# In layer 1 of a convolution-and-Mamba stack, ScalarE copies a projection right after its matmuls, and the pause comes after the copies

## The chip, the core and the metric

The kernel runs on one NeuronCore of one Trainium2 chip. A core has five engines that each work through their own instructions in order: TensorE (PE, matrix products; its weight loads are listed as PEld), VectorE (DVE), ScalarE (ACT), GpSimd (POOL) and SyncE (SP, which here issues the DMAs). They wait for each other by semaphores. The metric is the device time of one execution in microseconds (us), lower is better.

## The reference

The input x has the shape (8, 192, 56, 56). Four layers follow, each of the form x = x + layer(group_norm(x)):

```
x = x + L0(gn(x))    # involution, 5x5 taps made from the pixel itself
x = x + L1(gn(x))    # layer norm, three Mamba slices of 64 channels (d_inner 512), layer norm, projection
x = x + L2(gn(x))    # Mamba, d_inner 384
x = x + L3(gn(x))    # Mamba, d_inner 384
```

The change is in layer 1. There the 192 channels are split into three slices of 64, all with the same weights, and each slice of each image is a sequence of 3136 tokens:

```
xi, z = split(x @ in_proj_W.T)                 # 512 each
xc  = silu(causal_conv4(xi) + conv_b)
dbl = xc @ x_proj_W.T                          # 4 for dt, 16 for B, 16 for C
dt  = softplus(dbl[:, :4] @ dt_proj_W.T + dt_proj_b)
h   = h * exp(dt * A) + (dt * xc) * B          # 16 states per channel, along the sequence
y   = (sum over states of h * C + xc * D) * silu(z)
out = y @ out_proj_W.T
```

dbl, the projection of xc, is what the changed step makes: 36 rows that hold B, C and the 4 inputs of dt.

## The kernel before

A sequence is cut into 7 chunks of T = 448 tokens. In layer 1 a **job** is one slice (0, 1, 2) of one chunk of one image: 8 x 7 x 3 = 168 jobs. A job has 4 groups j of 128 channels with 4 **units** each (a unit q has 4 of the 16 states of each channel), 16 units in all, numbered m = 0 to 15 in the job. Layers 2 and 3 have 56 jobs of 12 units each. For each unit (loop at the end of `ssm_layer`):

- ACT makes the decays exp(dt * A) in PSUM, in two halves of two instructions each (`decays`, L749). There are two decay buffers, so the first half for unit k + 1 can't begin before the first scan of unit k is over.
- The inputs (dt * xc) * B are made by POOL for odd units (`inputs_by_pool`, L768) and by DVE for even ones (`inputs_by_vector`, L774), which reads a row b that PE spreads over the partitions (`spread_b`, L743).
- DVE runs two scans (`scan`, L778), one per half. ACT then copies the last column away for the next chunk (`keep`, L782).
- POOL multiplies with C in place (`readout`, L787). It can't begin before the keep has read the last column.
- PE adds up the states (`reduce`, L796; at the first unit of a group also xc * D, L793). DVE multiplies with silu(z) once per group (`gated`, L812).

While job i runs through its units, the background work of job i + 1 is laid between them: convolution and input projection on PE with ACT copies (L613), silu of xc and z (L616, L597, with table loads), the output projection of job i - 1 (L1076, copied by ACT in L1081), the **projection of xc** on PE (`xproj`, L621, four matmuls of two passes each), its two copies on ACT (`xproj_out`: L625 into `dbl`, L626 into `parts` as bf16), what bf16 left over of B (`left_of_b` L632 and L633, `part_of_b` L637), the matmuls of dt with their copies (`delta` L655, `delta_out` L660), the stores of B and C (`rows_out` L643), softplus (L663), and so on.

This background work is a list of `Step`s. A step has matmuls, a rest (the copies), a `left` and a cost. `Steps.run` first calls the rests that are pending until only `left` of them remain; then it issues the step's matmuls and puts its rest among the pending ones, or, for a step without matmuls, calls its rest at once. So a rest is issued when a later step flushes it. `pause` has left = 9 and flushes nothing; `flushed` has left = 0 and flushes all; both issue nothing themselves.

`places` deals the steps out over the 32 places of a job: places 2m and 2m + 1 belong to unit m. The steps come in stretches with bounds. The stretch that begins with the projection of xc has places 8 to 17 when the job being prepared is of slice 0 or 2, and 8 to 13 when it is of slice 1. At each place the room is the average of the cost that is left; steps are put there while room is over 0, each step takes its cost off it, and what a step took too much is a debt at the next places. In the unit's code the even place stands ahead of the first scan and of the first half of the decays for the next unit:

```
bg.run(plan[2 * m])
nothing(k - 3, more > 0)
load_when_free(k)
scan(k, 0)
if k + 1 < n_units:
    decays(k + 1, 0)
```

The odd place stands ahead of the second scan, the keep and the second half of the decays. `nothing` (L802) issues dummy matmuls that add zeros to the unit's sum, up to three in a unit, except in the last unit of a group; `more` is 3 less the rounded-up cost of those steps of the unit's two places that have matmuls.

Of the kernel before, what the change touches and what calls it, by code (L numbers as in the profile page):

```python
# [49 lines left out]
def pause(cost=1.0):  # L50
    return Step(None, lambda: None, 9, cost)


def settle(cost=2.0):

    step = Step(None, lambda: None, 0, cost)
    step.settles = True
    return step


def flushed(cost=1.0):

    return Step(None, lambda: None, 0, cost)
# [23 lines left out]
def conv_mamba_stack(ctx: ExitStack, tc: tile.TileContext, a, out):  # L87
# [16 lines left out]
    def mm_tile():  # L104
        return banks.mm.tile([128, 512], F32, tag="mm", name="mm")
# [481 lines left out]
    def table_block(ops):  # L587
        ops()
        nc.scalar.preload_act_table_set(EXP_SET)  # L589

    def with_gates(ops, u):


        def all_ops():
            ops()
            if u is not None:
                nc.scalar.activation(u.zs, u.zs, AF.Silu)  # L597

        table_block(all_ops)

    def project_steps(pool, w, u, conv_mm, conv_cost, running=None, meanwhile=()):


        nd, rank = w.nd, w.rank
        nk = rank + 2 * NS

        def conv(j):
            if j == 0:
                u.xc = pool.tile([128, nd, T], F32, tag="xc", name="xc", bufs=2)
            u.cps[j] = conv_mm(j)  # L610

        def conv_out(j):
            nc.scalar.activation(u.xc[:, j, :], u.cps[j][:, :T], AF.Identity, bias=w.convb[:, j : j + 1])  # L613

        def silu():
            with_gates(lambda: nc.scalar.activation(u.xc, u.xc, AF.Silu), running)  # L616

        def xproj():
            u.ps = mm_tile()
            for j in range(nd):  # L620
                nc.tensor.matmul(u.ps[:nk, :T], lhsT=w.xproj[:, j, :], rhs=u.xc[:, j, :], start=(j == 0), stop=(j == nd - 1))  # L621

        def xproj_out():
            u.dbl = pool.tile([44, T], F32, tag="dbl", name="dbl", bufs=2)
            nc.scalar.copy(u.dbl[:nk, :], u.ps[:nk, :T])  # L625
            nc.scalar.copy(u.parts[:NS, :], u.ps[:NS, :T])  # L626


        def left_of_b(m):
            u.left[m] = mm_tile()  # L630
            rows = NS if m == 0 else 96
            nc.tensor.matmul(u.left[m][:NS, :T], lhsT=ident[:NS, :NS], rhs=u.dbl[:NS, :], start=True, stop=False)  # L632
            nc.tensor.matmul(u.left[m][:NS, :T], lhsT=minus[:rows, m, :], rhs=u.parts[:rows, :], start=False, stop=True)  # L633

        def part_of_b(m):
            p0 = 32 * m + 32
            nc.scalar.copy(u.parts[p0 : p0 + NS, :], u.left[m][:NS, :T])  # L637

        def rows_out():

            u.bc = dram.tile([NS, 2, T], F32, tag="bc", name="bc", bufs=3)
            for c in range(2):
                nc.sync.dma_start(out=u.bc[:, c, :], in_=u.dbl[c * NS : c * NS + NS, :])  # L643

        def row_in(c, q):

            u.rows[c, q] = pool.tile([128, T], F32, tag=f"rows{c}", name="rows", bufs=4)
            by_n = u.bc.rearrange("(n q) c t -> n q c t", q=NQ)[:, q, c]
            nc.sync.dma_start(out=u.rows[c, q], in_=by_n.unsqueeze(0).to_broadcast([32, 4, T]))

        u.rows, u.row_in = {}, row_in

        def delta(j):
            u.dps[j] = mm_tile()
            nc.tensor.matmul(u.dps[j][:, :T], lhsT=w.dtw[:, j * 128 : (j + 1) * 128], rhs=u.dbl[:nk, :], start=True, stop=True)  # L655

        def delta_out(j):
            if j == 0:
                u.dt = pool.tile([128, nd, 2, T], F32, tag="dt", name="dt")
            nc.scalar.activation(u.dt[:, j, 0, :], u.dps[j][:, :T], AF.Identity, bias=w.dtb[:, j : j + 1])  # L660

        def softplus():
            table_block(lambda: nc.scalar.activation(u.dt[:, :, 0, :], u.dt[:, :, 0, :], AF.Softplus))  # L663

        def x_again(j):
            u.xps[j] = mm_tile()
            nc.tensor.matmul(u.xps[j][:, :T], lhsT=ident, rhs=u.xc[:, j, :], start=True, stop=True)  # L667

        def dtx(j):
            nc.vector.tensor_mul(u.dt[:, j, 1, :], u.dt[:, j, 0, :], u.xps[j][:, :T])  # L670

        def store(j):
            u.ops[j] = dram.tile([128, 2, T], F32, tag="ops", name="ops", bufs=8)
            nc.sync.dma_start(out=u.ops[j], in_=u.dt[:, j])

        u.ops, u.cps, u.dps, u.xps, u.left = {}, {}, {}, {}, {}
        deltas = [Step(lambda j=j: delta(j), lambda j=j: delta_out(j), 1) for j in range(nd)]

        stores = [Step(lambda j=j: x_again(j), lambda j=j: dtx(j), 1 if j > 1 else 9) for j in range(nd)]
        return (  # L680
            [Step(lambda j=j: conv(j), lambda j=j: conv_out(j), 1, conv_cost) for j in range(nd)]
            + [settle()], [Step(None, silu, 0, 0.3, block=True), *meanwhile] + [Step(xproj, xproj_out, 9, nd)] * (nd == 3),
            ([Step(xproj, xproj_out, 0, nd), pause()] if nd == 4 else [Step(None, lambda: None, 2, 3.5)])
            + [Step(lambda: left_of_b(0), lambda: part_of_b(0), 0, 1.3)] + deltas[:1] + [Step(None, rows_out, 2)] + deltas[1:2]
            + [Step(lambda: left_of_b(1), lambda: part_of_b(1), 1, 1.3)] + deltas[2:]
            + [settle()], [Step(None, softplus, 0, 0.3, block=True)] + stores[:2],
            [Step(None, lambda: store(0), 0)] + stores[2:3] + [Step(None, lambda: store(1), 1)]
            + stores[3:] + [Step(None, lambda j=j: store(j), nd - 1 - j) for j in range(2, nd)]
        )
# [295 lines left out]
    def mamba_jobs(pool, w):  # L985
# [3 lines left out]
        for ck in cks:  # L989
# [50 lines left out]
            for i in range(3):  # L1040

                def prepare(u, *beside, i=i, ck=ck, norm=norm):
                    def conv_mm(j):
                        pm = mm_tile()
                        for k in range(2):
                            nc.tensor.matmul(  # L1046
                                pm[:, :T], lhsT=w.inconv[:, k, j * 128 : (j + 1) * 128],
                                rhs=ck.xs[:, i, 2 - 2 * k : 2 - 2 * k + T], start=(k == 0), stop=(k == 1),
                            )
                        return pm  # L1050

                    convs, *others, stores = project_steps(pool, w, u, conv_mm, 2, *beside)
                    if i == 0:
                        stores = stores + [Step(None, lambda: chunks.fetch_next(ck), 2)]
                        if ck.place == 0:
                            convs = norm() + convs
                    return convs, *others, stores
# [34 lines left out]
    def dense_jobs(pool, w, layer):  # L1092
# [3 lines left out]
        for ck in cks:  # L1096
# [11 lines left out]
            def prepare(u, *beside, c=c, ck=ck, in_mm=in_mm):  # L1108
# [17 lines left out]
                def conv_mm(j):  # L1126
# [3 lines left out]
                    return pm  # L1130

                convs, *others = project_steps(pool, w, u, conv_mm, 4, *beside)
                return (
                    [Step(None, gnorm, 2)]
# [116 lines left out]
```

## Time and profile before

| what | us |
|---|---|
| median of 3 runs | 24955.37 (24948.31 to 24965.5) |
| the profiled execution, its time | 24963.74 |
| the profiled execution, its span | 24961.9 |
| layer 1 in it, first to last scan instruction and what hangs on them | 1607 to 17034 |
| busy in the span: PE | 21153.9 |
| DVE | 22616.8 |
| ACT | 17043.4 |
| POOL | 23597.2 |

The profile is of one execution. A page gives the busy time of each engine, and groups of instructions by line of the kernel: so many, busy time, mean duration in ns, and the idle time just ahead of them with what ended it. A timeline lists instructions in order of time: start and duration in us, engine, line, operation, what it writes and reads, and in brackets how long the engine had been idle before it and what released it. Rows of the same kind are merged (x3 is three instructions in a row). A fp32 matmul appears as two passes. A list of waits gives, for engine and line, what was waited for, the sum, the count and the longest. A row of stretches gives busy time (and number of instructions) of PE, PEld, DVE, ACT and POOL, then PE's granted clock (1.00 is full speed), the share of the DMA engines, and GB/s.

The costliest lines are DVE's scans (L778, 15905.1 us busy), POOL's readouts (L787, 14739.8), ACT's decays (L749, 10254.0) and POOL's inputs (L768, 8038.6).

### The profile page before, as it was taken

What the parts mean: (1) busy time and instruction counts of PE and PEld (TensorE: products, weight loads), DVE (VectorE), ACT (ScalarE), POOL (GpSimd) and SP (SyncE); (2) the same over time, 40 slices, a digit from 0 to 9 for tenths busy, and PEclk for the clock granted to TensorE, in tenths of its full rate; (3) what the DMA queues carried; (4) which work ended last, traced back from release to release, by engine and by line L of the source; (5) the groups of instructions that cost most, each with busy time, mean ns of one, the idle gap of its engine ahead of it and who ended that gap; (6) DMA issues with size and microseconds to landing.
All of it is one profiled execution on the core that took longest, in us unless ns stands there. A gap on an engine that the chain in (4) does not pass through costs nothing.

```text
span 24961.9 us, 237862 instructions
## 1 busy us (share of the span) xinstructions
PE 21153.9 (85%) x74220; PEld 6587.3 (26%) x74220; DVE 22616.8 (91%) x15661; ACT 17043.4 (68%) x32578; POOL 23597.2 (95%) x6996
## 2 busy tenths in 40 slices
PE   8988888888888888888888888888888888888888
PEld 2222222222222222222222222222333332333332
DVE  8989999999999999999999999997999998999998
ACT  2247777777767777777777777776777776777776
POOL 6679999999999999999999999998999998999999
PEclk9987777777777777777777777778888888888888
DMA  4433333333333333333333333333444443444443
GB/s 110 110 108 123 121 123 123 121 121 124 124 122 121 123 123 123 122 123 122 121 125 123 121 122 122 125 122 112 140 132 139 139 138 121 140 141 143 142 141 127
DMA packets 1184899, 3132.97 MB, mean 126 GB/s; under 512 B 163756, under 2 KB 446404, under 8 KB 1183496
## 3 DMA queue, kind: packets, MB, share of 16 engines
q1 hardware_dynamic: 1180824, 3116.70, 38.2%
q8 instruction: 582, 9.54, 0.2%
q14 instruction: 693, 5.68, 0.1%
q10 hardware_dynamic: 2800, 1.06, 0.0%
HBM read 2399.92 MB, written 555.55 MB: 118 GB/s over the span
## 4 chain that ended last, share of the span: by engine, by line
DVE 35%; PE 24%; ACT 17%; issue 11%; POOL 7%; DMA 4%; SPq 1%; DVEq 0%; POOLq 0%; ACTq 0%
DVE uhg L778 24%; ACT da L749 8%; DVE uhg L774 7%; PE y L796 4%; POOL uhg L787 4%; PE mm L655 4%; DMA rows<-bc 2%; PE y L802 2%; POOL uhg L768 2%; ACT L589 2%; PE y L793 2%; PE mm L632 2%; DMA rep<-ops 2%; ACT zs L597 1%; PE mm L429 1%
## 5 line engine op out<-in xcount | busy, mean ns | idle before, releaser
L778 DVE TENSOR_TENSOR_SCAN uhg<-da,uhg 128x898 f32<-128x898 f32 x8064 | 15905.1, 2009 | 1279.9 <-ACT da L749 1276.6
L787 POOL TENSOR_TENSOR uhg<-uhg,rows 128x1792 f32<-128x1792 f32 x4032 | 14739.8, 3676 | 275.4 <-ACT carry L782 267.4
L749 ACT ACTIVATE da<-rep,k 128x448 f32<-128x448 f32 x16128 | 10254.0, 636 | 1669.3 <-DVE uhg L778 1291.5
L768 POOL TENSOR_TENSOR uhg<-rep,rows 128x1792 f32<-128x1792 f32 x2016 | 8038.6, 3987 | 481.6 <-DMA rows<-bc 212.7
L796 PE MATMUL y<-uhg,k 128*32 128x448 f32 x32256 | 4780.6, 669 | 757.6 <-POOL uhg L787 755.3
L774 DVE TENSOR_TENSOR uhg<-rep,b 128x1792 f32<-128x1792 f32 x2016 | 4025.5, 1997 | 468.8 <-PE b L743 424.1
L782 ACT COPY carry<-uhg 128x4 f32<-128x4 f32 x4032 | 787.3, 195 | 3547.9 <-DVE uhg L778 3464.2
L793 PE MATMUL y<-xc,w_d 128*128 128x448 f32 x2016 | 1485.7, 832 | 1390.0 <-DVE zs L812 1388.3
L802 PE MATMUL y<-w_d,k 128*128 128x448 f32 (+1 forms) x5276 | 2496.8, 581 | 0.0
L796 PEld LDWEIGHTS y<-uhg,k 128*32 128x32 f32 x32256 | 695.9, 117 | 3858.8 <-issue 2203.8
L655 PE MATMUL mm<-dbl,w_dt 36*128 36x448 f32 (+1 forms) x2016 | 1501.2, 858 | 155.0 <-ACT k L637 155.0
L1102 PE MATMUL mm<-v,w_in 96*128 96x448 f32 x2688 | 1464.8, 677 | 170.1 <-ACT zs L694 71.1
L802 PEld LDWEIGHTS y<-w_d,k 128*128 128x128 f32 x5276 | 1050.9, 214 | 1480.4 <-issue 1452.5
L1046 PE MATMUL mm<-xs,k 128*128 128x448 f32 x2688 | 1229.7, 592 | 112.4 <-ACT zs L694 100.5
L1129 PE MATMUL mm<-xin,w_conv 128*128 128x448 f32 x2688 | 1077.9, 543 | 1.0 <-ACT xin L696 0.9
L441 DVE TENSOR_TENSOR prod<-mm,shifted 128x448 f32<-128x448 f32 x1680 | 928.6, 611 | 141.2 <-PE mm L429 63.5
L632 PE MATMUL mm<-dbl,k 16*16 16x448 f32 x1120 | 687.8, 702 | 422.7 <-ACT dbl L625 422.7
L667 PE MATMUL mm<-xc,k 128*128 128x448 f32 x2016 | 971.4, 592 | 30.8 <-DVE dt L670 29.7
L793 PEld LDWEIGHTS y<-xc,w_d 128*128 128x128 f32 x2016 | 443.3, 258 | 2056.5 <-DVE zs L812 1392.8
L1064 PE MATMUL mm<-xs,k 64*128 64x448 f32 x1344 | 861.6, 750 | 109.0 <-ACT zs L694 109.0
L743 PE MATMUL b<-k,k 96*128 96x448 bf16 x2016 | 832.2, 413 | 126.8 <-DVE uhg L774 126.6
L449 POOL TENSOR_TENSOR x<-x,one 96x448 f32<-96x448 f32 x560 | 631.1, 1134 | 265.9 <-DVE one L441 248.4
(138 smaller groups left out, 19672.2 us busy)
## 6 DMA issues: line engine op xcount, KB each, us to landing
rep<-ops SPq DMA_DIRECT2D x4032, 448.0 KB, 5.9
ops<-dt SPq DMA_DIRECT2D x1008, 448.0 KB, 3.3
rows<-bc SPq DMA_DIRECT2D x1792, 224.0 KB, 6.2
shifted<-xpad SPq DMA_DIRECT2D x672, 179.0 KB, 4.5
xg<-stream SPq DMA_DIRECT2D x168, 336.0 KB, 3.8
xr<-stream SPq DMA_DIRECT2D x168, 336.0 KB, 5.3
stream<-xr SPq DMA_DIRECT2D x112, 336.0 KB, 3.4
xs<-xg SPq DMA_DIRECT2D x224, 112.0 KB, 2.3
```

Of the source, the lines that this page charges most:

```text
L632: nc.tensor.matmul(u.left[m][:NS, :T], lhsT=ident[:NS, :NS], rhs=u.dbl[:NS, :], start=True, stop=False)
L655: nc.tensor.matmul(u.dps[j][:, :T], lhsT=w.dtw[:, j * 128 : (j + 1) * 128], rhs=u.dbl[:nk, :], start=True, stop=True)
L749: nc.scalar.activation(t[:, 64 + 449 * r : 512 + 449 * r], reps[k // NQ][:, 2 * h + r, 0, :], AF.Exp, scale=w.neg_a[:, j * NR + 2 * h + r, ...
L768: nc.gpsimd.tensor_mul(uhg[k][:, :, 1:], reps[k // NQ][:, :, 1, :], b)
L774: nc.vector.tensor_mul(uhg[k][:, :, 1:], reps[k // NQ][:, :, 1, :], b)
L778: nc.vector.tensor_tensor_scan(v, banks.da[h][:, 63:961], v, 0.0, ALU.mult, ALU.add)
L787: nc.gpsimd.tensor_mul(v, v, us[i].rows[1, q].unsqueeze(1).to_broadcast([128, NR, T]))
L793: nc.tensor.matmul(ys[k // NQ][:, :T], lhsT=w.dd[:, j, :], rhs=us[i].xc[:, j, :], start=True, stop=False)
L796: nc.tensor.matmul(y[32 * r : 32 * r + 32, :T], lhsT=fold, rhs=uhg[k][:, r, 1:], start=False, stop=(q == NQ - 1))
L802: nc.tensor.matmul(ys[k // NQ][:, : nd * 112], lhsT=zeros, rhs=w.dd.rearrange("p j e -> p (j e)")[:, : nd * 112], start=False, stop=False,)
L1046: nc.tensor.matmul(pm[:, :T], lhsT=w.inconv[:, k, j * 128 : (j + 1) * 128], rhs=ck.xs[:, i, 2 - 2 * k : 2 - 2 * k + T], start=(k == 0), st ...
L1102: nc.tensor.matmul(pm[:, :T], lhsT=w.inw[:, k, m * 128 : (m + 1) * 128], rhs=ck.v[:, k, :], start=(k == 0), stop=(k == NCT - 1),)
```

## The change

In the list that `project_steps` returns, for the four-group form of layer 1 alone, the step of the projection gets cost 1.0 in place of 4, a `flushed()` of cost 1.0 is put behind it, and the pause behind that gets cost 3.0 in place of 1.0:

```
-            ([Step(xproj, xproj_out, 0, nd), pause()] if nd == 4 else [Step(None, lambda: None, 2, 3.5)])
+            ([Step(xproj, xproj_out, 0, 1.0), flushed(), pause(3.0)] if nd == 4 else [Step(None, lambda: None, 2, 3.5)])
             + [Step(lambda: left_of_b(0), lambda: part_of_b(0), 0, 1.3)] + deltas[:1] + [Step(None, rows_out, 2)] + deltas[1:2]
             + [Step(lambda: left_of_b(1), lambda: part_of_b(1), 1, 1.3)] + deltas[2:]
             + [settle()], [Step(None, softplus, 0, 0.3, block=True)] + stores[:2],
```

`flushed` calls the pending rest, here the two copies L625 and L626, which before were called by the next step with matmuls, the first `left_of_b`. The sum of the three costs is 5 both times. No operation of the computation is added, left out or changed; since `more` is worked out from the costs, the number of `nothing` matmuls beside the projection follows from them.

More of the change, by code (lines that the diff above doesn't have):

```diff
@@ L682, in project_steps @@
             + [settle()], [Step(None, silu, 0, 0.3, block=True), *meanwhile] + [Step(xproj, xproj_out, 9, nd)] * (nd == 3),
-            ([Step(xproj, xproj_out, 0, nd), pause()] if nd == 4 else [Step(None, lambda: None, 2, 3.5)])
+            ([Step(xproj, xproj_out, 0, 1.0), flushed(), pause(3.0)] if nd == 4 else [Step(None, lambda: None, 2, 3.5)])
             + [Step(lambda: left_of_b(0), lambda: part_of_b(0), 0, 1.3)] + deltas[:1] + [Step(None, rows_out, 2)] + deltas[1:2]
```

## The prediction

> **What bounds the kernel now.** I read the page first, then layer 1 alone (1607 to 17034 us), because the edited line runs for `nd == 4`, which only layer 1 has. First the page's busy line, then layer 1 as one stretch (PE, PEld, DVE, ACT, POOL, granted clock, DMA), then the waits of POOL and DVE inside it:
>
> ```profile
> PE 21153.9 (85%) x74220; PEld 6587.3 (26%) x74220; DVE 22616.8 (91%) x15661; ACT 17043.4 (68%) x32578; POOL 23597.2 (95%) x6996
> ...
> 1607.00:17034.00 15427.00, 12939.79 (x40112) 3728.61 (x40112) 14128.32 (x8554) 10953.91 (x20959) 15070.15 (x4046) 0.77 0.36 122
> ...
> POOL uhg L787 <- ACT carry L782: 220.9, 195, 4.0
> ...
> DVE uhg L778 <- ACT da L749: 742.3, 394, 3.8
> DVE uhg L774 <- PE b L743: 369.0, 222, 2.7
> ```
>
> POOL is busy 15070 of 15427 us, so at most some 357 us can be won here. DVE, at 14128, follows closely, and POOL already waits 220.9 us for scans (through the small keep copy L782). So the two engines limit each other in turn: what makes scans late costs nothing while POOL still has readouts to do, and everything once it has run out. I read POOL's lag from the timelines as the start of each readout L787 minus the end of its second scan, by unit m of the 16 in a job and by the slice (0, 1, 2) that the job prepares. The medians are 5.5 us at m = 5 and 2.7 at m = 10 in slice-0 jobs, but 0.31 (the smallest that occurs: none left) at m = 14 of slice 1 and at m = 4, 10 and 12 of slice 2. The lag is used up twice in every three jobs.
>
> Then the place itself, in a job that prepares slice 2 (timelines of PE, ACT, DVE and POOL; start, duration; the value in brackets is idle time before):
>
> ```profile
> 5017.43 4.99 PE L1076 MATMUL mm<-zs,w_out 128*64 128x448 f32 x8
> 5022.35 0.96 PE L796 MATMUL y<-uhg,k 128*32 128x448 f32 x8
> 5023.24 3.20 PE L621 MATMUL mm<-xc,w_x 128*36 128x448 f32 x8
> ...
> 5023.07 0.52 ACT L1081 COPY y<-mm 64x448 f32<-64x448 f32 x1
> 5023.81 1.31 ACT L749 ACTIVATE da<-rep,k 128x448 f32<-128x448 f32 x2 [0.22 <-DVE uhg L778]
> 5025.05 0.18 ACT L757 COPY uhg<-carry 128x4 f32<-128x4 f32 x1
> 5025.72 0.20 ACT L782 COPY carry<-uhg 128x4 f32<-128x4 f32 x1 [0.49 <-DVE uhg L778]
> ...
> 5028.97 0.52 ACT L625 COPY dbl<-mm 36x448 f32<-36x448 f32 x1
> 5029.40 0.52 ACT L626 CAST k<-mm 16x448 bf16<-16x448 f32 x1
> ...
> 5021.74 5.86 DVE L778 TENSOR_TENSOR_SCAN uhg<-da,uhg 128x898 f32<-128x898 f32 x3 [2.84 <-ACT da L749]
> ...
> 5025.02 7.30 POOL L787 TENSOR_TENSOR uhg<-uhg,rows 128x1792 f32<-128x1792 f32 x2
> ```
>
> This is unit 4. The projection of xc (L621) ends at 5026.4; its copies (L625, L626) come 2.5 us later, when nobody has to wait for PE. The decays at 5023.81 are what the third scan of the DVE row, which starts at 5025.59, needs.
>
> **The change part by part.** *Where the copies go.* In `places` (L821) the stretch has 13.9 of cost, before (4 + 1 + 8.9) and after (1 + 1 + 3 + 8.9). Over 10 places (slices 0 and 2) room is 1.39 at place 8, over 6 places (slice 1) 2.32. The projection now takes 1.0 of it, so room is left and `flushed()` falls into the same place 8. So the copies are issued straight behind their matmuls, ahead of the decays for unit 5 on ACT. From place 11 (10 in slice 1) on the plan is what it was, since the sums are equal.
>
> *What ACT pays.* Both copies keep their duration: L625's start to L626's end is 0.95 us. They now wait for L621, and behind them are queued the decays of unit 5, the small copy L757 and the keep of unit 4 (L782). Slice-2 example: L621's end 5026.42, release 0.04 (L633's end to L637 at another place of this job), copies 0.95, decay pair to scan 1.34 (5020.40 to 5021.74): the scan starts at 5028.75 instead of 5025.59, D = 3.16 us late. When PE is quicker, D shrinks. In a slice-0 job:
>
> ```profile
> 3455.33 3.22 PE L1076 MATMUL mm<-zs,w_out 128*64 128x448 f32 x8
> 3459.37 3.20 PE L621 MATMUL mm<-xc,w_x 128*36 128x448 f32 x8
> ...
> 3462.49 0.52 ACT L1081 COPY y<-mm 64x448 f32<-64x448 f32 x1
> ```
>
> L621 is done at 3462.57, ACT at 3463.01, so only the copies themselves are in the way: 3463.01 + 0.95 + 1.34 = 3465.30 against 3465.04, D = 0.26. I took D so for 166 jobs. Slice 0 (55): 0.26 in 29, 3.16 in 23, 81.7 us in all. Slice 1 (55): 0.26 to 2.86, mostly 0.3 to 1.6, 59.7. Slice 2 (56): 3.16 in 50, 161.1.
>
> *What sets D is PE's clock.* L1076 takes 3.22 us at a granted clock of 1.00 (stretch 3455.3 to 3458.5) and 4.99 at 0.64 (5017.4 to 5022.4). The job of 3364.73 shows a half-clock stretch behind a wait of 1.61 us:
>
> ```profile
> 3360.79 1.02 PE L793 MATMUL y<-xc,w_d 128*128 128x448 f32 x2 [1.61 <-DVE zs L812]
> 3361.74 1.37 PE L796 MATMUL y<-uhg,k 128*32 128x448 f32 x8
> ...
> 3364.73 5.31 PE L1076 MATMUL mm<-zs,w_out 128*64 128x448 f32 x8
> ```
>
> [...]
>
> *What is won.* PE's wait at L632 for L625 (350.2 us over layer 1) goes. But the next step on that chain, the second delta matmul, waits for L637, which stands on ACT behind the decays of unit 7, and these wait for a scan. So that chain moves with DVE and gives nothing back in slices 0 and 2. In slice 1 the left-over copies now also leave ACT's queue ahead of unit 6's decays, and DVE's later waits there come from PE (L774 for L743, 64.0 us at m = 8) and from the softplus behind PE-bound copies (64.8 at m = 8): about 2.3 us a job that covers D up to that. I take slice 1 at nothing. Its bounds: a gain of 1.4 us a job (the second delta and left matmuls at full instead of half clock, 2 x 0.9 less 0.4), -77, and the whole of D, +60.
>
> *Two more dummy matmuls.* `nothing` (L802) is asked for by `more`, which counts the costs of steps with matmuls: at m = 4 that was 4 (none), it is 1 (two). Each is 1.02 us at full clock, 167 x 2.04 = 341 us of PE. They lie where PE waited for L625 or stands idle before the second delta; the b row (L743) for DVE is later by one of them, 5027.7 against a reader at 5030.7. At nothing, then; without that cover, DVE would be at most 1.0 us later a job, 170 us. `pause(3.0)` issues nothing. On SP the two stores of dbl (L643) can go 2.5 us sooner; the next load behind them waits for other things.
>
> *POOL.* The readout of unit 4 waits for the delayed keep. In slice 2 it starts 0.28 us after the keep does (median), so POOL stands for nearly D at once. In slice 0 the 2.4 us of lag at m = 10 takes up some of D, until m = 14 of the next job, where none is left.
>
> *Sum.* 81.7 + 161.1 + 0 = 243 us on the profiled execution's 24963.74 gives 25207; the median shown is 8 us lower, so 25200. Bounds: D at 0.26 in all jobs of slices 0 and 2 (29 us) with the slice-1 gain (-77): -48; D at 3.16 in all of them (351) and 60 in slice 1: +411. I take the phases as the trace has them, since the waits that cause them lie ahead of the edited place.
>
> **The rivals.** (a) POOL's lag hides slice 0 as well: 161 us, 25115. For it: 5.5 us of lag at m = 5. Against: none at m = 14 of the next job. (b) Faster: the dummies and the closed gap at L632 keep PE at full clock through units 5 to 9. DVE's waits at m = 8 to 10 add up to 523 us over the three slices; less D at 0.26 (43 us) this could give 480, and half of the waits gives 24955 - 262 + 43 = 24735. It decides if PE's idle time ahead of the second delta stays under 1.6 us, the shortest that a half-clock stretch followed in the rows above. Against: the first left matmul now ends at about 5031.9, the delta can't start before 5038.6, and between them are 2.3 us of work: 4.4 us idle. In the slice-0 job it comes to 3.9. (c) The change does what its name says: copies one place behind, after unit 5's decays. Then no scan is late; only the keep is, by 2 us, POOL waits sooner instead of later in slice 2, and the time stays near 24955. Against: the room of 0.39 at place 8. (d) The added lateness puts the out projection on half clock in nearly all jobs, slice 1 too: the upper bound, 25365.
>
> **How the numbers follow.** Forecast 0.66, (a) 0.16, (b) 0.08, (c) 0.05, (d) 0.05. A change of 0.2% (50 us) is about what can be told from none. Slower: forecast, (a) and (d), 0.66 + 0.16 + 0.05 = 0.87, less 0.02 for forecasts with quick phases, 0.85; same: (c) and those 0.02, 0.07; faster: (b), 0.08. The range leaves out (b), (c) and the far ends: 25000 to 25380.
>
> **What would show it.** L621 of layer 1 named as what ACT waits for before L625, some 250 us in all, at most 3.0 a time; DVE's wait for L749 up from 742 to about 1000; POOL's wait for L782 up from 221 to 400 or more; L802 up by some 670 instructions; L632's wait for L625 gone. Wrong, if POOL's waits rise much less than DVE's (then (a)), if layer 1's granted clock rises well above 0.77 (then (b)), or if L625 comes after unit 5's decays (then (c)).

## The result, and the profile after

The changed kernel takes 25087.99 us (median of 4 runs, 25058.35 to 25099.4) where the kernel before takes 24957.25 (4 runs): 1.005 times as long, 95% interval 1.0035 to 1.0065. It is slower by 131 us, inside the range of 25000 to 25380, at about half of the forecast loss of 243.

The page's busy lines, then layer 1's waits (ACT, DVE, POOL and PE, from 1607 to 17160 us: what waited, for what, sum, count, longest) of the changed kernel:

```profile
PE 21030.2 (84%) x74888; PEld 6618.8 (26%) x74888; DVE 22633.5 (90%) x15661; ACT 17027.2 (68%) x32578; POOL 23610.2 (94%) x6996
...
ACT dbl L625 <- PE mm L621: 111.2, 85, 2.9
...
DVE uhg L778 <- ACT da L749: 866.5, 499, 3.8
DVE uhg L774 <- PE b L743: 345.5, 237, 2.7
...
POOL uhg L787 <- ACT carry L782: 331.2, 259, 3.7
...
PE mm L655 <- ACT k L637: 642.7, 167, 5.5
```

No engine has more work that matters: DVE and POOL are as busy as before. What grew are waits, in the order that the prediction walked through: ACT now waits for the projection (L621) ahead of its copy L625, DVE's scans wait 124 us more for the decays, POOL waits 110 us more for the keeps. PE's wait at L632 for L625 (350.2 us before) is gone, and a wait for L637 ahead of the delta matmuls has grown in its place (155.0 before).

One unit 4 in a job that prepares slice 2 (timelines of PE, ACT, DVE and POOL):

```profile
3664.17 1.02 PE L793 MATMUL y<-xc,w_d 128*128 128x448 f32 x2 [1.95 <-DVE zs L812]
...
3668.45 4.91 PE L1076 MATMUL mm<-zs,w_out 128*64 128x448 f32 x8
3673.30 0.96 PE L796 MATMUL y<-uhg,k 128*32 128x448 f32 x8
3674.18 3.20 PE L621 MATMUL mm<-xc,w_x 128*36 128x448 f32 x8
3677.31 1.02 PE L802 MATMUL y<-w_d,k 128*128 128x448 f32 x2
...
3674.07 0.52 ACT L1081 COPY y<-mm 64x448 f32<-64x448 f32 x1
3677.42 0.53 ACT L625 COPY dbl<-mm 36x448 f32<-36x448 f32 x1 [2.83 <-PE mm L621]
3677.85 0.52 ACT L626 CAST k<-mm 16x448 bf16<-16x448 f32 x1
3678.27 1.29 ACT L749 ACTIVATE da<-rep,k 128x448 f32<-128x448 f32 x2
...
3672.74 3.94 DVE L778 TENSOR_TENSOR_SCAN uhg<-da,uhg 128x898 f32<-128x898 f32 x2 [2.84 <-ACT da L749]
3679.67 2.03 DVE L778 TENSOR_TENSOR_SCAN uhg<-da,uhg 128x898 f32<-128x898 f32 x1 [2.98 <-ACT da L749]
...
3679.86 3.68 POOL L787 TENSOR_TENSOR uhg<-uhg,rows 128x1792 f32<-128x1792 f32 x1 [3.10 <-ACT carry L782]
```

This is the predicted chain. L625 stands straight behind L1081 and ahead of the decays. ACT waits 2.83 us for PE, the scan of unit 5 comes 2.98 us late, and POOL, which has no lag here, stands for 3.10 us at once. The row L802 is the first of the two added dummies.

How often it happens is another matter. The groups of L1076 (the output projection just ahead of L621) in layer 1, before and after:

```profile
L1076 PE MATMUL mm<-zs,w_out 128*64 128x448 f32 x1344 | 689.2, 667 | 0.0
```

```profile
L1076 PE MATMUL mm<-zs,w_out 128*64 128x448 f32 x1344 | 557.2, 559 | 0.0
```

A pass takes 559 ns on average in place of 667: in more jobs PE was at full clock there (3.22 us for the eight passes at a granted clock of 1.00, against some 5 where part of them ran at half clock, as the 4.91 at 0.64 in the job above), and was done sooner. Of the 166 jobs, 158 had a quick L1076, where 93 had one before.

I measured the lateness D from the scans: the time from the first scan of unit 4 to the first of unit 5 is 3.86 us in every job of the kernel before, and what exceeds that is D. Its sum over 166 jobs, and what the rest of the job (all other units) gained or lost, in us:

| prepared slice | D forecast from the trace before | D measured | rest of the job | together |
|---|---|---|---|---|
| 0 (55 jobs) | 82 | 7 | -8 | -1 |
| 1 (55) | 60, taken as covered | 70 | -29 | 41 |
| 2 (56) | 161 | 65 | +14 | 79 |
| all | 243 counted | 142 | -23 | 119 |

The two profiled executions differ by 135.7 us in span. 119 are these jobs (the two jobs left out are 2 us shorter), 12.9 lie before layer 1's first scan and 5.7 after its last. The change doesn't touch those other layers, and the first scan starts anywhere from 1584.8 to 1620.6 us in the profiles of this case, so the 12.9 is scatter between executions.

The column "rest of the job" hides larger moves. In slice 0, units 8 and 9 are 67 us shorter in all, but unit 1 is 45 us longer: in 28 of the 55 jobs it takes 7.5 us or so instead of 5.8 (3 jobs before), because DVE waits there for the b row from PE. One such job: DVE in unit 1, then the stretch ahead of unit 1 and unit 1 itself (granted clock 0.50 and 0.84, the third number from the end):

```profile
3468.32 2.02 DVE L774 TENSOR_TENSOR uhg<-rep,b 128x1792 f32<-128x1792 f32 x1 [1.71 <-PE b L743]
...
3459.00:3464.60 5.60, 5.60 (x10) 1.26 (x13) 5.60 (x3) 3.60 (x8) 4.08 (x2) 0.50 0.87 267
3464.60:3472.20 7.60, 7.60 (x29) 2.91 (x22) 5.89 (x5) 3.87 (x9) 7.60 (x4) 0.84 0.56 198
```

In the kernel before, 23 slice-0 jobs were at half clock for part of L1076 (granted 0.59 or 0.60 over it); in the changed kernel none is (1.00 in all), but 28 are at half clock in units 0 and 1. So the half-clock stretch in part moved rather than went away.

### The profile page after: what moved, and what is told of

The parts are those of the page before. It is cut to its first block, busy times and chain, and to the rows that moved or that the text cites. A ratio compares the mean times of both kernels' runs of the same rounds, so it can differ in the third digit from the quotient of the medians.

```text
span 25097.6 us, 239198 instructions
## 1 busy us (share of the span) xinstructions
PE 21030.2 (84%) x74888; PEld 6618.8 (26%) x74888; DVE 22633.5 (90%) x15661; ACT 17027.2 (68%) x32578; POOL 23610.2 (94%) x6996
## 4 chain that ended last, share of the span: by engine, by line
DVE 31%; PE 25%; ACT 16%; issue 11%; POOL 10%; DMA 5%; SPq 1%; DVEq 0%; POOLq 0%; ACTq 0%
DVE uhg L778 21%; POOL uhg L787 7%; ACT da L749 7%; DVE uhg L774 6%; PE y L796 5%; PE mm L655 3%; POOL uhg L768 3%; DMA rows<-bc 3%; PE y L793 2%; PE y L802 2%; DMA rep<-ops 2%; ACT L589 2%; PE mm L429 1%; PE mm L632 1%; PE mm L1064 1%
## 5 line engine op out<-in xcount | busy, mean ns | idle before, releaser
L787 POOL TENSOR_TENSOR uhg<-uhg,rows 128x1792 f32<-128x1792 f32 x4032 | 14753.4, 3679 | 399.9 <-ACT carry L782 391.2
L749 ACT ACTIVATE da<-rep,k 128x448 f32<-128x448 f32 x16128 | 10251.6, 636 | 1679.1 <-DVE uhg L778 1307.1
L796 PE MATMUL y<-uhg,k 128*32 128x448 f32 x32256 | 4744.9, 664 | 748.4 <-POOL uhg L787 745.7
L774 DVE TENSOR_TENSOR uhg<-rep,b 128x1792 f32<-128x1792 f32 x2016 | 4028.9, 1998 | 441.2 <-PE b L743 396.0
L782 ACT COPY carry<-uhg 128x4 f32<-128x4 f32 x4032 | 787.0, 195 | 3564.1 <-DVE uhg L778 3452.7
L802 PE MATMUL y<-w_d,k 128*128 128x448 f32 (+1 forms) x5944 | 2777.7, 572 | 0.0
L793 PE MATMUL y<-xc,w_d 128*128 128x448 f32 x2016 | 1511.8, 845 | 1409.1 <-DVE zs L812 1408.9
L655 PE MATMUL mm<-dbl,w_dt 36*128 36x448 f32 (+1 forms) x2016 | 1380.8, 792 | 643.0 <-ACT k L637 642.7
L796 PEld LDWEIGHTS y<-uhg,k 128*32 128x32 f32 x32256 | 694.6, 117 | 3930.2 <-issue 2286.3
L802 PEld LDWEIGHTS y<-w_d,k 128*128 128x128 f32 x5944 | 1140.7, 207 | 1618.3 <-issue 1591.6
L793 PEld LDWEIGHTS y<-xc,w_d 128*128 128x128 f32 x2016 | 448.9, 261 | 2064.0 <-DVE zs L812 1364.8
L743 PE MATMUL b<-k,k 96*128 96x448 bf16 x2016 | 797.0, 395 | 161.4 <-DVE uhg L774 161.3
L1102 PEld LDWEIGHTS mm<-v,w_in 96*128 96x128 f32 x2688 | 580.8, 232 | 1080.7 <-issue 444.9
```

What stands on the lines that cost most here:

```text
L749: nc.scalar.activation(t[:, 64 + 449 * r : 512 + 449 * r], reps[k // NQ][:, 2 * h + r, 0, :], AF.Exp, scale=w.neg_a[:, j * NR + 2 * h + r, ...
L774: nc.vector.tensor_mul(uhg[k][:, :, 1:], reps[k // NQ][:, :, 1, :], b)
L787: nc.gpsimd.tensor_mul(v, v, us[i].rows[1, q].unsqueeze(1).to_broadcast([128, NR, T]))
L793: nc.tensor.matmul(ys[k // NQ][:, :T], lhsT=w.dd[:, j, :], rhs=us[i].xc[:, j, :], start=True, stop=False)
L796: nc.tensor.matmul(y[32 * r : 32 * r + 32, :T], lhsT=fold, rhs=uhg[k][:, r, 1:], start=False, stop=(q == NQ - 1))
L802: nc.tensor.matmul(ys[k // NQ][:, : nd * 112], lhsT=zeros, rhs=w.dd.rearrange("p j e -> p (j e)")[:, : nd * 112], start=False, stop=False,)
```

## The experiments

The theory is lateness: the copies hold back unit 5's decays, and most of that reaches the end. The rival is that the two added dummy matmuls a job, and what they do to PE's clock, make the time.

### Copies alone

```
-            ([Step(xproj, xproj_out, 0, 1.0), flushed(), pause(3.0)] if nd == 4 ...
+            ([Step(lambda: (xproj(), xproj_out()), lambda: None, 0, nd), pause()] if nd == 4 ...
```

> The copies stand right behind the projection's matmuls as in the changed kernel, but the step keeps its cost of 4, so the two dummy matmuls a job are not issued. Lateness theory (the copies hold back the decays of unit 5, and this alone makes the time): slower than before by what DVE loses at unit 4, 140 us if the PE clock around the output projection is as in the changed kernel, up to 243 us if it is as before: 25100 to 25200, L802 at 5276 instructions. Dummy theory (the added matmuls and what they do to the clock make the time): as before, 24957 within 50 us.

Measured: 25117.26 us against 24953.36, 1.0066 (1.0053 to 1.008), 164 us slower. D by slice is 7, 68 and 84 us, 159 in all. DVE's wait for the decays in layer 1:

```profile
DVE uhg L778 <- ACT da L749: 882.5, 508, 3.8
```

Without any added matmul the loss is there, so the rival falls as the cause of the loss. L1076 is quick here too (572 ns a pass), so it isn't the dummies that quickened it.

### Dummies alone

```
-            ([Step(xproj, xproj_out, 0, 1.0), flushed(), pause(3.0)] if nd == 4 ...
+            ([Step(xproj, xproj_out, 0, 1.0), pause(4.0)] if nd == 4 ...
```

> The projection's cost is 1 as in the changed kernel, so the two dummy matmuls a job are issued, but the copies stay with the first left-over step, as before. Lateness theory: no lateness at unit 4, so not slower than before; at best faster by what a better clock gives at units 8 to 10, some 50 to 70 us: 24890 to 24960. Dummy theory: the changed kernel's time, 25090 within 50 us.

Measured: 24910.86 us, 0.9982 (0.9973 to 0.999), 42 us faster. No unit 4 is longer. DVE's wait for the b row in layer 1, as the group of L774 has it (idle before, in us, behind the bar), fell from 369.0 to 286.1:

```profile
L774 DVE TENSOR_TENSOR uhg<-rep,b 128x1792 f32<-128x1792 f32 x1358 | 2714.2, 1999 | 315.4 <-PE b L743 286.1 <-DMA rep<-ops 29.1
```

The dummies help a little. If the two simply add, the change is a loss of 164 and a gain of 42: 122, where 131 were measured. That they add is not shown: the intervals of the change (87 to 162 us) and of the copies alone (132 to 200) overlap.

### The copies twice

```
             nc.scalar.copy(u.dbl[:nk, :], u.ps[:nk, :T])
             nc.scalar.copy(u.parts[:NS, :], u.ps[:NS, :T])
+            if nd == 4:
+                nc.scalar.copy(u.dbl[:nk, :], u.ps[:nk, :T])
+                nc.scalar.copy(u.parts[:NS, :], u.ps[:NS, :T])
```

> The changed kernel with both copies issued twice in layer 1 (the same values again), 0.95 us more of ACT ahead of the decays of unit 5 in each of 167 jobs. Lateness theory: lateness at unit 4 grows by 0.95 us a job and all of it reaches the end: 159 us more than the changed kernel, 25190 to 25260. If POOL's lag hides lateness at unit 4 for the most part: under 40 us more, 25090 to 25130.

Measured: 25231.42 us, 1.0112 (1.0098 to 1.0125), 0.62% or some 150 us more than the changed kernel. Line numbers behind the insertion are 3 higher:

```profile
3390.69 0.53 ACT L625 COPY dbl<-mm 36x448 f32<-36x448 f32 x1 [2.88 <-PE mm L621]
3391.12 0.52 ACT L626 CAST k<-mm 16x448 bf16<-16x448 f32 x1
3391.54 0.52 ACT L628 COPY dbl<-mm 36x448 f32<-36x448 f32 x1
3391.97 0.52 ACT L629 CAST k<-mm 16x448 bf16<-16x448 f32 x1
3392.39 1.29 ACT L752 ACTIVATE da<-rep,k 128x448 f32<-128x448 f32 x2
```

The added 0.85 us a job are 142 us in all (159 were expected, of 0.95), and the time grew by about as much. That agreement is in part luck: D grew from 142 to 367 us, more than the copies themselves, because in 46 of 56 slice-2 jobs PE was now at half clock at L1076 again (616 ns a pass over all jobs, 559 in the changed kernel), while layer 1 grew by some 148 us over the changed kernel (15663.3 against 15515.2, first to last unit). So two thirds of the added lateness reach the end, and POOL's lag doesn't hide most of it. Of the lateness in all, 72% is left in layer 1's time here and 82% in the changed kernel.

### Half of the output projection left out

In layer 1 the kernels leave out the first two of the four groups of L1076:

```
-                        for j in range(4):
+                        for j in range(2, 4):
                             nc.tensor.matmul(u.ps[:64, :T], lhsT=w.outw[:, j, :], ...
```

> The same half of layer 1's output projection left out of the kernel before, as the one to compare with. PE is not the bound, so the time hardly changes: 24900 to 24960 by both theories; what it differs from 24957 by is what a shorter projection does to the PE clock.

> Leaves out half of layer 1's output projection: two of the four groups' matmuls (L1076), so PE reaches the projection of xc 1.6 us earlier at full clock and up to 2.6 us earlier at half. Otherwise the kernel with copies right behind the matmuls and no added dummies. If D is set by when PE ends the projection, the copies hardly wait any more and only their own 0.26 us a job is left, some 45 to 70 us beside the same cut in the kernel before, in place of 164. If instead the copies cost by their place on ACT alone, whatever PE does, the difference stays near 164.

Measured: 24948.64 us (0.9998, 0.9989 to 1.0007) with the cut in the kernel before, 25047.4 us (1.0038, 1.0025 to 1.0052) with the cut and early copies. The early copies cost 99 us here (58 to 139), 164 (132 to 200) without the cut. So their price seems to hang on when PE gets to the projection, as D does, which falls from 159 to 125 us; the two intervals just touch, and 45 to 70 was missed. D is still 125 us, because L621 ends 1.1 us behind the end of unit 4's first scan in the 40 slice-2 jobs at half clock (2.66 in such jobs without the cut, of which there are 16), which is late enough. In slice 1, with the cut, POOL holds PE up ahead of L621 in all 55 jobs (L796 waits for L787; 27 jobs without the cut), so L621's end moved from 0.95 to only 0.37 (medians).

### One place behind the matmuls

With the dummies, and the copies behind unit 5's first decays:

```
-            ([Step(xproj, xproj_out, 0, 1.0), flushed(), pause(3.0)] if nd == 4 ...
+            ([Step(xproj, xproj_out, 0, 1.0), pause(1.4), flushed(0.6), pause(2.0)] if nd == 4 ...
```

> The two dummy matmuls as in the changed kernel, and the copies one place further back, behind the decays of unit 5 and ahead of the keep of unit 4 on ACT. Lateness theory: the scans of unit 5 are on time again; only the keep is late by up to 2 us, which POOL feels only where it has no lag: 24890 to 24990. Dummy theory: 25090 within 50 us.

The same without the dummies:

```
+            ([Step(xproj, xproj_out, 0, 2.4), flushed(0.6), pause(2.0)] if nd == 4 ...
```

> Copies one place behind the matmuls, as in the fastest run so far, but the projection's cost is 2.4, so that the two dummy matmuls are not issued. If the gain of 74 us there is the dummies' 43 and some 30 from the earlier left-over chain: 24900 to 24945. If it is all the dummies': 24957 within 30. If it is all the early copies': 24880 within 20.

Measured: 24879.3 us with the dummies, 0.997 (0.9959 to 0.9981), and 24888.5 without, 0.9971 (0.996 to 0.9983). Both beat the kernel before, by 74 and 66 us, and the changed one by about 200. The first is 11 us below its expected range of 24890 to 24990; the second fits the last of its three cases (all the early copies'). The time from unit 4's first scan to unit 5's is 3.86 us in every job again. The dummies make no difference that these intervals can tell; the early copies bring it. With the dummies, unit 4 (ACT) and then PE and DVE further on in the same job:

```profile
3354.07 1.31 ACT L749 ACTIVATE da<-rep,k 128x448 f32<-128x448 f32 x2 [0.22 <-DVE uhg L778]
3355.32 0.18 ACT L757 COPY uhg<-carry 128x4 f32<-128x4 f32 x1
3355.40 0.52 ACT L625 COPY dbl<-mm 36x448 f32<-36x448 f32 x1
...
3365.70 1.86 PE L655 MATMUL mm<-dbl,w_dt 36*128 36x448 f32 x2 [5.40 <-ACT k L637]
...
3378.36 2.00 DVE L774 TENSOR_TENSOR uhg<-rep,b 128x1792 f32<-128x1792 f32 x1
```

The same place of the same job in the kernel before (PE, then DVE):

```profile
3383.06 1.86 PE L655 MATMUL mm<-dbl,w_dt 36*128 36x448 f32 x2 [1.69 <-ACT k L637]
...
3399.07 2.02 DVE L774 TENSOR_TENSOR uhg<-rep,b 128x1792 f32<-128x1792 f32 x1 [2.67 <-PE b L743]
```

The decays come first and no scan is late. PE now idles 5.40 us ahead of the second delta, and its passes are at half clock behind that (1.86 us for two, where two of the first delta took 1.02); but it is back at full clock sooner, and DVE's wait of 2.67 us for b is gone. The stretches from 15 to 30 us behind the end of unit 4's first scan, in a slice-0 and a slice-2 job, before and then one place behind (PE's granted clock is the third number from the end):

```profile
3478.20:3493.20 15.00, 15.00 (x44) 4.51 (x44) 12.13 (x7) 11.65 (x20) 15.00 (x5) 0.66 0.32 110
3386.40:3401.40 15.00, 15.00 (x40) 4.24 (x40) 11.02 (x7) 11.67 (x20) 15.00 (x5) 0.56 0.33 113
```

```profile
3461.30:3476.30 15.00, 14.08 (x56) 4.43 (x56) 13.85 (x10) 12.32 (x23) 15.00 (x5) 0.92 0.35 126
3369.00:3384.00 15.00, 14.08 (x57) 4.44 (x57) 13.79 (x10) 12.27 (x23) 15.00 (x5) 0.91 0.36 126
```

POOL's wait for the keeps in layer 1 falls to 140.4 us, from 220.9 before:

```profile
POOL uhg L787 <- ACT carry L782: 140.4, 96, 3.2
```

Not all that is won stays. With the dummies, units 8 and 9 of slices 0 and 2 are 211 us shorter in all than before, but unit 1 of slice 0 is 84 us longer and unit 11 of slice 2 56 us, where DVE now waits for PE (L774 for L743, and L563, of the layer norm, for L557).

## Why the prediction was right, and where not

- **Where the copies go** was right. They are not one place behind but in the same place 8, as the room of 0.39 said, and that is the whole loss: one place further on, the kernel is about 200 us faster.
- **What ACT pays** was right for a job. In the one shown, L621 ends at 3677.38; with 0.04 + 0.95 + 1.34 the scan was to start at 3679.71, and it started at 3679.67. (The copies held ACT for 0.85 us rather than 0.95, and the decays took a little longer to the scan.)
- **The sum of D** is the term that was mis-sized. "I take the phases as the trace has them, since the waits that cause them lie ahead of the edited place" was the step that failed: slices 0 and 2 measured 72 us where 243 were summed. L1076 went from 667 to 559 ns a pass. That this comes mostly with the early copies is shown by the copies alone (572) and by the copies one place behind without dummies (562), against 643 with the dummies alone. What the traces show of the way: in the trace before, the granted clock is 1.00 or 0.50 in 1582 stretches (it falls to 0.50 at 3362.15 us and is back at 1.00 at 3368.98, for one), and these begin on a grid, whole multiples of 3413.3 ns apart to within 0.01 us; so do the 1502 of the changed kernel. Most slice-0 jobs of the kernel before wait the same 3.10 us at L793, ahead of L1076. L793 then starts 1.96 to 2.04 us past a point of that grid in the 23 with a slow L1076, and 1.55 to 1.82 us past it in the 29 with a quick one. In the changed kernel 27 slice-0 jobs have this wait, L793 starts 1.62 to 1.83 us past the grid in them, and all are quick. So in these jobs some 0.3 us lie between slow and quick (medians 2.02 and 1.68), and a job whose length changes a little shifts all that follow. Why the jobs settle where they do was not shown.
- **The number** was in the range in part by luck. 171 us too many were counted in slices 0 and 2, and 41 us too few in slice 1. The 131 measured lie nearer to the 161 of rival (a) than to the forecast, but not for its reason: it takes the 161 us of D in slice 2 as paid in full, and D there was 65.
- **Slice 1 at nothing** was wrong: of its 70 us only 29 came back. The covers that were named are real (its units 6 to 8 are 30 us shorter) but smaller.
- **What is won, at nothing** was wrong for the early copies as such. Without lateness they are worth 66 us. That is the mechanism of rival (b): the clock comes back sooner, by units 8 and 9. Its condition was wrong, though: it asked for less than 1.6 us of idle time ahead of the second delta; in slices 0 and 2 there were 5.40 (median; 0.16 in slice 1), and the gain came all the same. In the changed kernel layer 1's granted clock rose from 0.77 to 0.79 only.
- **The dummies at nothing** was wrong by 42 us when alone. Beside copies one place behind it was right within the intervals; beside the changed kernel's own copies it is open, as said above.
- **POOL** was right in the main: its wait for the keeps rose nearly as much as DVE's for the decays (110 and 124 us), which was the sign against rival (a), and most of the lateness is left in layer 1's time. For slice 0 alone, which is what (a) is about, it isn't settled: in the changed kernel there were only 7 us to hide. With the copies twice there were 54, and slice-0 jobs are only 16 us longer than before, but other units of these jobs moved by more than that, so what the lag hid can't be read off. The signs to look for were right in kind and too big where they hung on D: ACT's wait at L625 111 us (250 forecast), DVE's at L749 866 (1000), POOL's at L782 331 (400 or more). L802 has 668 more instructions, and L632's wait is gone.
- **D at 0.26 in every job**, the 43 us that rival (b) counts for all 166, was off too: by 88, where the forecast's 243 was off by 112. The forecast was off because most output projections became quick. The 43 was off because a quick one doesn't mean D = 0.26: in slice 1 L1076 was quick in every job before, and the prediction's own D there adds up to 60. In the changed kernel a job costs 0.13 us in slice 0, but 1.4 in 27 of the 48 slice-2 jobs with a quick L1076, and mostly 1.1 to 1.5 in slice 1. The prediction's row of a half-clock stretch behind a wait of 1.61 us has its like after the change: the 4.91 us of L1076 above (granted clock 0.64) stand behind a wait of 1.95 us at L793.

## What to carry to other kernels

A copy that is moved up to right behind its matmuls can make its engine wait for them, and what is queued behind it waits too (2.83 us of ACT and 2.98 of DVE in the job shown): put it behind the work that the critical engine needs next; here one place later was enough, and worth about 200 us. Work out from the planner's own arithmetic where a step lands, since a cost of 1.0 against room for 1.39 put this one into the wrong place. And take a lateness that hangs on a clock's state in the old trace as a range, not as a number: here the edit changed the state (L1076 from 667 to 559 ns a pass), and of 243 us summed for slices 0 and 2, 72 were measured.

## What the runs showed that I had not expected

A longer wait did not mean a longer stretch at half clock. With the copies one place behind, PE waits 5.40 us ahead of L655 and runs at half clock afterwards, as it did before behind 1.69 (1.86 us for two passes both times); but the granted clock 15 to 30 us behind the end of unit 4's first scan is 0.91 to 0.92 in place of 0.56 to 0.66. Why it recovers sooner stays open. And the price of one and the same edit (copies in front of the decays) depends on a state that it changes itself: 142 us of lateness in one kernel, 367 with 0.85 us more of copies.
